# Moving VectorE's maxima ahead of its transposes, and with them the order of a transfer queue, in a two-layer cross-attention kernel

## The chip, the cores and the metric

The kernel runs on one core of a Trainium2 chip. The metric is the device time of one launch in microseconds (us). Engines go by the names of the profile: PE is the matrix engine TensorE (PEld its weight loads), DVE is VectorE, ACT is ScalarE, POOL is GpSimd, and SP is SyncE, which here issues nearly all DMA transfers. Each engine works through its own instructions in order, and waits on semaphores for the others.

## What is computed

The reference, cut to its parts (16 batches, 256 rows of width 256, all float32):

```
x = x + L0_xattn(ctx, LN(x))   # 8 heads of 128; queries from LN(LN(x)); keys and values
                               # over the 512 rows LN(ctx) and LN(LN(x))
x = x + L0_ffn(LN(x))          # 256 -> 1024 -> 256, GELU; both weights get an update
                               # per batch, products of tokens 1..16 of the batch
x = x + L1_xattn(LN(x), ctx)   # one head of 256, keys and values from ctx
x = x + L1_moe(LN(x))          # 8 experts (gate, up, down, width 256); weights by a
                               # sigmoid zone, with a fallback to the top two
```

## The kernel before, in words

**Two kinds of work.** The first attention is laid out head by head: 16 batches of 8 heads give 128 heads, and the loop at L1239 to L1279 runs a step n for each (and two more). Everything else of a batch is its *tail*: the FFN, the second attention and the routing (`chain`, L332, and `route`, L584). The experts (`experts`, L1174) begin to run near the end of the loop. Tails are generators: each `yield` ends a unit, and says how many microseconds of PE time should pass before the next one. The step calls `gap()` (L114), which runs units of tails that are due by a clock (`Clock.pe`) that sums the modelled time of matmuls. So the order on every engine is fixed when the program is built; at run time the engines only wait for each other. The chain of batch b-1 joins in at head 2 of batch b.

**A head.** Its steps are spread over several steps of the loop, so that PE always has another head's work:

- `s0q(n+1)` (L801) and `s0k(n+1)` (L814): query and key projections `pq`, `pk`; their results `qT`, `kT` are evicted by ACT (`evict`, L774), or by DVE while the clock says that ACT is taken.
- `s1(n)` (L832): for both halves of the queries the scores `sc`, on DVE the maxima `nm` (L841), on ACT the exp into `pr` (L847).
- `s1_scale(n)`: reciprocals on DVE (L854), scaling of `pr` on POOL (L855).
- `s2(n)` (L857): DVE transposes `pr` in blocks of 32 into `tb` (L863, a single buffer), and SP writes `tb` to DRAM: `hop`, 512 KB (L867).
- `s2_fetch(n)` (L870): SP reads it back in another order, four transfers of 128 KB, into `pT` (L876, two buffers).
- `s3(n)` (L879): PE multiplies `pT` with the values into `po`, and DVE evicts it as `outT` (L893).

Step n of the loop calls, in this order: `s1(n)`, a gap, `s1_scale(n)`, `s2_fetch(n-1)`, `s0q(n+1)`, a gap, `s0k(n+1)`, gaps with `bulk` between them, `s3(n-2)`, a gap, `s2(n)`. `bulk` (L1010) advances the values' projection `pv` and `inputs(b+1)` (L714): the statistics, normalized rows (`cn`, `xn`) and, by DVE transposes and trips through DRAM (`hop_cin`, `hop_cn`, `hop_xn`, fetched into `raw`), the transposed inputs `kvT` of the next batch. It advances the inputs at heads 0 to 4.

**A tail, as far as the change touches it.** The output projection `px` (L351) is added to x (L354); statistics follow, and the reciprocal deviation `rs_b` on POOL (L262). DVE normalizes to `yb` (L267) and copies a few rows to `yp` (L373). SP writes 8 rows to DRAM (`ev_d`, two transfers of 4 KB, L375 and L376) and reads them back to all partitions, `ev`, 1 MB (L380): these are the weight rows from which the FFN's updated weights are made. Then `to_blocks` (L285 to L296) transposes `yb` on DVE and writes it to DRAM, `hop_yb` (256 KB), fetched by `from_blocks` (L299) in four transfers. After the FFN comes the second attention in the same manner: `yc` and its `hop_yc`, the queries' constants `rc` (two reductions on DVE, L488), the values `pv1` (L500), the queries `q1T` from the fetched `ycT` (L508), scores and exp, `pr1` through DRAM (`hop_pr`, `pr1T`), its copy `pT1` (L537), the product `po1`, statistics and `rs_d`. Last comes `row` (L557), which needs `rs_d`, and its own trip, for the routing and the experts.

Since SP has one queue for all of this, a fetch stands behind every transfer issued before it.

Of the kernel before, what the change touches and what calls it, by code (L numbers as in the profile page):

```python
# [16 lines left out]
ALU = mybir.AluOpType  # L17
# [12 lines left out]
def xattn_ffn_kernel(  # L30
# [10 lines left out]
    nc = tc.nc  # L41
    B, S, D = x.shape
# [7 lines left out]
    TC = S // P  # L50
# [13 lines left out]
    wk = ctx.enter_context(tc.tile_pool(name="work_c", bufs=1))  # L64
# [49 lines left out]
    def gap(least=0.8, stand=0.0):  # L114


        t = Clock.pe
        while Clock.pe - t < least:
            line[:] = [j for j in line if not j.done]
            if not line:  # L120
                return
            job = next((j for j in line if j.ready <= Clock.pe), None)
            if job is None:
                soon = min(j.ready for j in line)
                if soon > Clock.pe + stand:
                    return
                Clock.pe = soon
                continue
            job.unit()
        line[:] = [j for j in line if not j.done]  # L130
# [15 lines left out]
        out=before, in_=before, compare_op=ALU.is_gt, fill=0.0,  # L146
# [9 lines left out]
        out=below, in_=below, compare_op=ALU.is_gt, fill=0.0,  # L156
# [77 lines left out]
    g1 = keep.tile([P, D], F32, name="g1")  # L234
    g0 = keep.tile([P, 1], F32, name="g0")
# [49 lines left out]
    def to_blocks(pool, src, C, tag, bufs, name, most=None):  # L285
        tb = pool.tile(
            [P, C * D], F32, tag=tag, bufs=bufs, name=name, padded_shape=[P, most or C * D]
        )
        tb = tb.rearrange("p (m d c s) -> p m d c s", m=QP, d=DC, c=C)
        for c in range(C):  # L290
            nc.vector.transpose(  # L291
                tb.rearrange("p m d c s -> p d m c s")[:, :, :, c, :],
                src[:, c, 0:D].rearrange("p (d m r) -> p d m r", d=DC, m=QP),
            )
        hop = dram.tile([P, QP, DC * C * QB], F32, tag=f"{tag}{C}", name=f"hop_{name}")
        nc.sync.dma_start(hop, tb.rearrange("p m d c s -> p m (d c s)"))  # L296
        return hop
# [11 lines left out]
    SENT, LANDED = 6.5, 7.5  # L309
# [22 lines left out]
    def chain(b, A, behind):  # L332
# [37 lines left out]
        y = wk.tile([P, TC, D], F32, tag="y", name=f"yb_{b}")  # L370
        ln_apply(y, x_b, mv, rs)
        yp = wk.tile([32, NI, NA], F32, tag="yp", name=f"yp_{b}")
        nc.vector.tensor_copy(yp, y[0:32, 0, :].rearrange("p (a c) -> p c a", c=NI))  # L373
        ev_d = dram.tile([2 * NI, D], F32, tag="ev_d", name=f"ev_d_{b}")
        nc.sync.dma_start(ev_d[0:NI, :], y[1 : 2 * NI : 2, 0, :])  # L375
        nc.sync.dma_start(  # L376
# [6 lines left out]
        )  # L383
        landed = Clock.pe + 15.0
        plus_row(x_b, lasting["b2"])
        hop = to_blocks(wk, y, TC, "tbc", 1, f"yb_{b}_b")
        yield SENT
        yTb = raw_tile("yT", f"ybT_{b}")
        from_blocks(yTb, hop)
# [94 lines left out]
        hop = to_blocks(wk, y, TC, "tbc", 1, f"yc_{b}_b")  # L484
        pr = wk.tile([P, TC, S], F32, tag="pr1", name=f"pr1_{b}")
        rc = small.tile([P, TC], F32, tag="rc", bufs=2, name=f"rc_{b}")
        for c in range(TC):
            nc.vector.tensor_tensor_reduce(  # L488
                out=pr[:, c, :], in0=y[:, c, :], in1=g1, op0=ALU.mult, op1=ALU.add,
                scale=1.0, scalar=g0, accum_out=rc[:, c : c + 1],  # L490
            )
        yield SENT
        yTc = raw_tile("raw_c", f"ycT_{b}")
        from_blocks(yTc, hop)
        landed = Clock.pe + LANDED


        v1 = wk.tile([P, TC, D], F32, tag="v1", name=f"v1_{b}")
        for m in range(TC):
            pv = mm_tile(D, f"pv1_{b}_{m}")  # L500
            for d in range(DC):
                mm(pv, cT[:, d, ts(m, P)], WvT[:, d, :], start=(d == 0), stop=(d == DC - 1))
            evict(v1[:, m, :], pv, None, None)
            yield
        yield landed - Clock.pe
        q1T = wk.tile([P, DC, S], F32, tag="q1T", name=f"q1T_{b}")
        for m in range(DC):
# [27 lines left out]
        pT = wk.tile([P, TC, S], F32, tag="pT1", bufs=1, name=f"pT1_{b}")  # L535
        for m in range(TC):
            evict(pT[:, m, :], in_order(raw)[:, m], None, None)  # L537
        yield 2.5
        mv = mv_tile("d")
        for c in range(TC):  # L540
            ri = small.tile([P, 1], F32, tag="ri1", name=f"ri1_{b}_{c}")
# [9 lines left out]

        rs = ln_rstd(mv, "d")
        nc.sync.dma_start(out[b].rearrange("(c p) d -> p c d", p=P), x_b)
        yield 2.8
        while b >= 2 and not A.tails[b - 2].done:
            yield 0.4
        row = A.row[b] = wk.tile([P, TC, ROW], F32, tag="row", bufs=2, name=f"row_{b}")  # L557
# [136 lines left out]
    with ExitStack() as sh, ExitStack() as sa, ExitStack() as sf:  # L694
# [137 lines left out]
        def s1(n):  # L832

            b, h = divmod(n, H)
            qT, kT = heads[n]
            rows_ = []
            for c in range(TC):
                sc = psum.tile([P, J], F32, tag="sc", name=f"sc_{b}_{h}_{c}")
                mm(sc, qT[:, ts(c, P)], kT, start=True, stop=True)
                nm = small.tile([P, 1], F32, tag="nm", name=f"nm_{b}_{h}_{c}")  # L840
                nc.vector.tensor_reduce(nm, sc, AX.X, ALU.max, negate=True)  # L841
                rows_.append((sc, nm))
            heads[n] = []
            for c, (sc, nm) in enumerate(rows_):
                pr = wh.tile([P, J], F32, tag="pr", bufs=4, name=f"pr_{b}_{h}_{c}")
                sm = small.tile([P, 1], F32, tag="sm", name=f"sm_{b}_{h}_{c}")
                nc.scalar.activation(pr, sc, AF.Exp, bias=nm, accum_out=sm)  # L847
                heads[n].append((pr, sm))
# [21 lines left out]
        def s2_fetch(n):  # L870

            b, h = divmod(n, H)
            pT = wh.tile([P, QP, TC, P], F32, tag="pT", name=f"pT_{b}_{h}")
            from_ = heads[n].rearrange("(a r) m f -> m r a f", r=QB)
            for m in range(QP):
                nc.sync.dma_start(pT[ts(m, QB)].rearrange("r a c f -> r a (c f)"), from_[m])  # L876
            heads[n] = pT

        def s3(n):  # L879

            b, h = divmod(n, H)
            pT, v = heads.pop(n), A.v[b, h // HG]
            o = wh.tile([P, S], F32, tag="outT", bufs=H + H // 2, name=f"outT_{b}_{h}")
            A.outT.setdefault(b, []).append(o)
            po = mm_tile(S, f"po_{b}_{h}")
            for j in range(JC):
                mm(
                    po, v[:, j, ts(h % HG, DH)],
                    pT.rearrange("p a c f -> p c a f")[:, :, :, ts(j, QB)],
                    start=(j == 0), stop=(j == JC - 1),  # L890
                )

            nc.vector.tensor_scalar(o, po, col("bv", h), None, ALU.add)  # L893
# [116 lines left out]
        def bulk(b, h):  # L1010
            if h == 0:
                if b == 0:
                    filling["turns"] = all_turns()
                filling["in"] = inputs(b + 1) if b + 1 < B else None
            if h == 2:
                filling["v1"] = values(b, 1)
            if h == 6:
                filling["v0"] = values(b + 1, 0) if b + 1 < B else None
            if b == 0:
                load_late(h)  # L1020
                for _ in range(2):
                    advance(filling["turns"])
            if 2 <= h <= 5:
                advance(filling["v1"])
            if h <= 4:
                advance(filling["in"])
            if h == 7 and b + 2 < B:
                load_in(b + 2)
            if h >= 6:
                advance(filling["v0"])  # L1030
                yield
                advance(filling["v0"])
            yield
# [205 lines left out]
        for n in range(NS + 2):  # L1239
            b, h = divmod(n, H)  # L1240
            if h == 2 and b > 0:
                last = add_chain(b - 1, last)
            more = bulk(b, h) if n < NS else None
            if n < NS:
                s1(n)
            if n == NS - 4:
                sf.close()
                open_front()
                rest = Job(experts(
                    lists,  # L1250
                    lambda g: g.part == 0 or B - 1 in A.tails and A.tails[B - 1].done,
                ))
                line.append(rest)
            if n == NS - 1:
                sa.close()
                open_last_layer()
            while behind_exp:
                behind_exp.pop()()
            stand = 2.0 if n >= NS - 1 else 0.0
            gap(stand=stand)  # L1260
            if n < NS:
                s1_scale(n)
            if 1 <= n <= NS:
                s2_fetch(n - 1)
            if n + 1 < NS:
                s0q(n + 1)
            gap(stand=stand)
            if n + 1 < NS:
                s0k(n + 1)
            gap(stand=stand)  # L1270
            advance(more)
            gap(stand=stand)
            advance(more)
            gap(stand=stand)
            if n >= 2:
                s3(n - 2)
            gap(stand=stand)
            if n < NS:
                s2(n)  # L1279
        line.remove(rest)  # L1280
        last = add_chain(B - 1, last)
        line.append(rest)
# [56 lines left out]
```

## Time and profile before

| | |
|---|---|
| median of 3 runs | 1907.38 us (1905.83 to 1913.34) |
| the profiled execution: its time, its span | 1906.59 us, 1904.8 us |
| mean granted clock of PE | 0.989 |
| PE busy | 1824.0 us, 96% of the span |
| PE weight loads, DVE | 1228.8 us (65%), 1226.8 us (64%) |
| ACT, POOL | 593.1 us (31%), 871.1 us (46%) |
| DMA | 336.92 MB, mean 177 GB/s; SP's queue took 47.1% of the 16 DMA engines' span |
| largest single transfers | `ev` 1024 KB (16 times), `hop` 512 KB (128 times), `pT` 128 KB (512 times) |

A row of groups names the source line, the engine, the operation with output and inputs, the tile shapes and the count; behind the first bar are busy time and mean nanoseconds of one, and behind the second the idle time of the engine just before such instructions, with what ended most of it. In a timeline the columns are start and duration in us, engine, line, operation, count (x2 is two run together), and in brackets a wait before it and its releaser. Engine SPq is the issue of a transfer by SP, not the transfer itself. All matmuls carry line L80, that of the helper that issues them, so they are told apart by their tiles.

### The profile page before, as it was taken

The page shows a single profiled execution, that of the slowest core. Times are in us where ns is not written, and L with a number is a line of the kernel's source. Part 1 is how long each engine was busy: PE and PEld are TensorE (multiplying, and loading weights), DVE is VectorE, ACT ScalarE, POOL GpSimd, SP SyncE. Part 2 cuts the span into 40 slices and gives each one's busy share as a digit, 9 for nine tenths or more (in the row PEclk, how much of TensorE's full clock was granted, in tenths as well). Part 3 has the DMA queues.
Part 4 walks back from the last instruction along what each step waited for, and adds up shares of the span by engine and source line. Part 5 has one row for each costly group of instructions (what it writes and reads, how often), then busy time and mean ns, then how long its engine had stood idle before and what let it go on. Part 6 is the DMA issues. An engine that isn't in the chain of part 4 may idle for free. (4 is left out here: it accounts for less than half of the span.)

```text
span 1904.8 us, 22785 instructions
## 1 busy us (share of the span) xinstructions
PE 1824.0 (96%) x6568; PEld 1228.8 (65%) x6568; DVE 1226.8 (64%) x3324; ACT 593.1 (31%) x1323; POOL 871.1 (46%) x996
## 2 busy tenths in 40 slices
PE   8999999999999999999999999999999999899996
PEld 4666666666666666666666666666666767566665
DVE  4466586757575757585857575858574767565654
ACT  3433334333333333333333333333333212111110
POOL 2132226343535353535353535353534275767666
PEclk9999999999999999999999999999999999999999
DMA  6553536464636463636363636363636587999996
GB/s 214 177 188 122 167 133 216 140 200 136 200 131 204 133 213 130 199 126 212 128 216 128 212 127 203 126 214 126 219 118 202 157 224 194 232 246 234 216 206 109
DMA packets 274638, 336.92 MB, mean 177 GB/s; under 512 B 31772, under 2 KB 227272, under 8 KB 272456
## 3 DMA queue, kind: packets, MB, share of 16 engines
q1 hardware_dynamic: 243736, 283.82, 47.1%
q0 software_dynamic: 30720, 51.54, 11.4%
q8 instruction: 55, 0.90, 0.2%
q14 instruction: 79, 0.65, 0.1%
q10 hardware_dynamic: 48, 0.01, 0.0%
HBM read 167.87 MB, written 167.38 MB: 176 GB/s over the span
## 5 line engine op out<-in xcount | busy, mean ns | idle before, releaser
L855 POOL TENSOR_SCALAR pr<-pr,ri 128x512 f32<-128x512 f32 x256 | 182.5, 725 | 664.0 <-DVE ri L854 662.0
L847 ACT ACTIVATE pr<-sc,nm 128x512 f32<-128x512 f32 x256 | 173.5, 682 | 578.1 <-DVE nm L841 575.4
L674 POOL DMA_INDIRECT slots_d<-row,at_slot x256 | 255.6, 998 | 68.2 <-issue 68.2
L80 PE MATMUL sc<-kT,qT 128*128 128x512 f32 x512 | 253.1, 618 | 33.2 <-ACT kT L780 33.2
L80 PE MATMUL po<-pT,v 128*128 128x256 f32 x1024 | 243.3, 380 | 4.0 <-DMA pT<-hop 3.6
L1165 POOL DMA_INDIRECT out_dram<-o,at x128 | 200.0, 1563 | 99.2 <-DVE o L1164 27.1
L80 PE MATMUL pk<-kvT,Wk_sb 128*128 128x512 f32 x512 | 240.6, 592 | 0.0
L80 PE MATMUL pv<-Wv_sb,kvT 128*128 128x512 f32 x512 | 239.1, 596 | 0.1
L80 PEld LDWEIGHTS po<-pT,v 128*128 128x128 f32 x1024 | 194.4, 190 | 67.0 <-issue 37.7
L863 DVE STREAM_TRANSPOSE tb<-pr 128x512 f32<-128x512 f32 x256 | 165.6, 684 | 34.9 <-DMA hop<-tb 34.9
L80 PEld LDWEIGHTS sc<-kT,qT 128*128 128x128 f32 x512 | 98.0, 197 | 108.7 <-issue 64.8
L841 DVE TENSOR_REDUCE nm<-sc 128x1 f32<-128x512 f32 x256 | 160.3, 662 | 4.8 <-PE sc L80 3.8
L893 DVE TENSOR_SCALAR outT<-po,cvec 128x256 f32<-128x256 f32 x128 | 60.0, 469 | 157.8 <-PE po L80 137.6
L80 PEld LDWEIGHTS pv<-Wv_sb,kvT 128*128 128x128 f32 x512 | 95.6, 190 | 98.4 <-issue 89.0
L80 PEld LDWEIGHTS pk<-kvT,Wk_sb 128*128 128x128 f32 x512 | 97.3, 190 | 67.8 <-issue 61.2
L80 PE MATMUL pd<-wx,hTd 128*128 128x256 f32 x512 | 125.8, 383 | 9.9 <-DVE hTd L1151 7.9
L80 PE MATMUL pq<-kvT,Wq_sb 128*128 128x256 f32 x512 | 131.9, 380 | 0.0
L1140 ACT ACTIVATE sg<-pg 128x384 f32<-128x384 f32 (+3 forms) x82 | 41.2, 503 | 290.6 <-PE pg L80 242.8
L80 PE MATMUL pg<-yTd,wx 128*128 128x384 f32 (+3 forms) x328 | 125.1, 504 | 3.6 <-issue 3.0
L80 PEld LDWEIGHTS pq<-kvT,Wq_sb 128*128 128x128 f32 x512 | 97.5, 191 | 42.9 <-issue 31.3
L80 PEld LDWEIGHTS pd<-wx,hTd 128*128 128x128 f32 x512 | 97.4, 192 | 41.8 <-DVE hTd L1151 8.7
L80 PE MATMUL pu<-yTd,wx 128*128 128x384 f32 (+3 forms) x328 | 124.4, 502 | 0.0
(191 smaller groups left out, 2703.2 us busy)
## 6 DMA issues: line engine op xcount, KB each, us to landing
hop<-tb SPq DMA_DIRECT2D x128, 512.0 KB
pT<-hop SPq DMA_DIRECT2D x512, 128.0 KB
ev<-ev_d SPq DMA_DIRECT2D x16, 1024.0 KB
rows<-slots_d SPq DMA_DIRECT2D x31, 397.5 KB
hop_rows_b<-rows_b SPq DMA_DIRECT2D x30, 384.0 KB
yTd<-hop_rows_b SPq DMA_DIRECT2D x120, 96.0 KB
rows<-slots_d SPq DMA_DIRECT2D x8, 530.0 KB
cin<-in_ctx_dram SPq DMA_DIRECT2D x16, 256.0 KB
```

Source lines behind the costliest of these rows:

```text
L80: nc.tensor.matmul(out, lhsT, rhs, **kw)
L674: ins = nc.gpsimd.indirect_dma_start(out=slots_d[part], out_offset=bass.IndirectOffsetOnAxis(ap=at_slot[:, c, e : e + 1], axis=0), in_=row ...
L841: nc.vector.tensor_reduce(nm, sc, AX.X, ALU.max, negate=True)
L847: nc.scalar.activation(pr, sc, AF.Exp, bias=nm, accum_out=sm)
L855: nc.gpsimd.tensor_scalar(pr, pr, ri, 1.0, ALU.mult, ALU.mult)
L863: nc.vector.transpose(tb[:, :, c, :], heads[n][c][0].rearrange("p (m f) -> p m f", m=QP))
L893: nc.vector.tensor_scalar(o, po, col("bv", h), None, ALU.add)
L1140: nc.scalar.activation(self.sg, self.pg, AF.Tanh, scale=0.5)
L1165: ins = nc.gpsimd.indirect_dma_start(out=out_rows[0 : sum(NTOKS[: self.part + 1]), :], out_offset=bass.IndirectOffsetOnAxis(ap=self.at[:, ...
```

## The change

Seven edits; the number of instructions of each kind stays what it was.

1. `s2(n-1)` is called in step n right after `s1(n)`, where before `s2(n)` ended step n. The maxima of head n so come ahead of the transposes of head n-1.
2. `s2_fetch(n-1)` moves from after `s1_scale(n)` to after `s3(n-2)`, near the end of the step.
3. `inputs` is advanced at heads 1 to 5 instead of 0 to 4.
4. The queries' constants `rc` are computed after the values `v1` (two units later), and the queries' `landed` time is set 1.5 later.
5. The product `po1` is due 4.0 instead of 2.5 after `pT1`.
6. The tail's `hop_yb` (transposes and write) comes ahead of `ev_d` and `ev` on DVE and SP.
7. In the last batch `row` is due 10.0 instead of 2.8 after `rs_d`.

In the built program one more thing follows from the clock: in twelve batches the two copies into `ydT` are DVE's instead of ACT's.

```diff
         nc.vector.tensor_copy(yp, y[0:32, 0, :].rearrange("p (a c) -> p c a", c=NI))
+        hop = to_blocks(wk, y, TC, "tbc", 1, f"yb_{b}_b")
         ev_d = dram.tile([2 * NI, D], F32, tag="ev_d", name=f"ev_d_{b}")
...
         landed = Clock.pe + 15.0
         plus_row(x_b, lasting["b2"])
-        hop = to_blocks(wk, y, TC, "tbc", 1, f"yb_{b}_b")
         yield SENT
...
         rc = small.tile([P, TC], F32, tag="rc", bufs=2, name=f"rc_{b}")
-        for c in range(TC):
-            nc.vector.tensor_tensor_reduce(
-                out=pr[:, c, :], in0=y[:, c, :], in1=g1, op0=ALU.mult, op1=ALU.add,
-                scale=1.0, scalar=g0, accum_out=rc[:, c : c + 1],
-            )
         yield SENT
         yTc = raw_tile("raw_c", f"ycT_{b}")
         from_blocks(yTc, hop)
-        landed = Clock.pe + LANDED
+        landed = Clock.pe + LANDED + 1.5
...
             evict(v1[:, m, :], pv, None, None)
             yield
+        for c in range(TC):
+            nc.vector.tensor_tensor_reduce(
...
         yield landed - Clock.pe
...
             evict(pT[:, m, :], in_order(raw)[:, m], None, None)
-        yield 2.5
+        yield 4.0
...
         nc.sync.dma_start(out[b].rearrange("(c p) d -> p c d", p=P), x_b)
-        yield 2.8
+
+        yield 2.8 if b < B - 1 else 10.0
...
-            if h <= 4:
+            if 1 <= h <= 5:
                 advance(filling["in"])
...
             if n < NS:
                 s1(n)
+            if 1 <= n <= NS:
+                s2(n - 1)
...
             if n < NS:
                 s1_scale(n)
-            if 1 <= n <= NS:
-                s2_fetch(n - 1)
...
             if n >= 2:
                 s3(n - 2)
+            if 1 <= n <= NS:
+                s2_fetch(n - 1)
             gap(stand=stand)
-            if n < NS:
-                s2(n)
```

More of the change, by code (lines that the diff above doesn't have):

```diff
@@ L504, in chain @@
             yield
+        for c in range(TC):
+            nc.vector.tensor_tensor_reduce(
+                out=pr[:, c, :], in0=y[:, c, :], in1=g1, op0=ALU.mult, op1=ALU.add,
+                scale=1.0, scalar=g0, accum_out=rc[:, c : c + 1],
+            )
         yield landed - Clock.pe
```

## The prediction, made before the changed kernel ran

> **What bounds the kernel now.** I read four views in this order: busy shares and groups, the waits of TensorE (PE), the timeline of one batch, and the window table where PE had waited. PE is busy 1824.0 of 1904.8 us, so only what makes PE wait, or slows its clock, moves the time. Its groups:
>
> ```profile
> L80 PE MATMUL sc<-kT,qT 128*128 128x512 f32 x512 | 253.1, 618 | 33.2 <-ACT kT L780 33.2
> L80 PE MATMUL po<-pT,v 128*128 128x256 f32 x1024 | 243.3, 380 | 4.0 <-DMA pT<-hop 3.6
> ```
>
> The last columns are the idle time before the group and what ended it. Scores wait 33.2 us for keys evicted by ScalarE; the weighted values wait 4.0 us although every head's `pT` goes out to DRAM and back. The waits, as sum, count, longest:
>
> ```profile
> PE sc L80 <- ACT kT L780: 33.2, 13, 2.8
> PE pd L80 <- DVE hTd L1151: 7.9, 2, 7.7
> PE po L80 <- DMA pT<-hop: 3.6, 4, 2.5
> PE po L80 <- ACT pT L778: 3.1, 4, 1.2
> ```
>
> The 13 waits are twelve of 2.2 to 2.8 us, one a batch from batch 4 on, always ahead of head 2's scores, and one of 1.5. In batch 9:
>
> ```profile
> 843.30 1.96 PE L80 MATMUL sc<-kT,qT 128*128 128x512 f32 x4
> ...
> 846.55 1.02 DVE L488 CUSTOM_DVE_ANT_0 pr<-yc,g,g 128x256 f32<-128x256 f32 x1
> 847.91 1.29 DVE L863 STREAM_TRANSPOSE tb<-pr 128x512 f32<-128x512 f32 x2
> 849.13 1.25 DVE L841 TENSOR_REDUCE nm<-sc 128x1 f32<-128x512 f32 x2
> 849.88 0.69 ACT L847 ACTIVATE pr<-sc,nm 128x512 f32<-128x512 f32 x1 [7.77 <-DVE nm L841]
> 851.57 0.69 ACT L780 ACTIVATE kT<-pk,cvec 128x512 f32<-128x512 f32 x1
> 852.32 1.98 PE L80 MATMUL sc<-kT,qT 128*128 128x512 f32 x4 [2.74 <-ACT kT L780]
> ```
>
> Head 1's scores are done by 845.3, but VectorE (DVE) first works off inputs, the constants (L488) and the transposes of head 0, and takes the maxima at 849.13. ScalarE stands in order behind its exp, so head 2's keys come 3.2 us after that and PE 2.74 us late. The releaser ACT is innocent; DVE's order is the cause.
>
> **The change, part by part.**
>
> *Maxima first, constants and inputs later: gain.* Built, the maxima of head n stand ahead of head n-1's transposes. In the odd batches what remains ahead of head 1's maxima is nine routing rows (2.27 us in batch 9), in the even ones less. The maxima then start about 2.9 us after the scores instead of 849.13-843.30 = 5.83; keys follow 3.19 us later (852.32-849.13), at 6.1; PE has work until 849.58, 6.3 after them. The wait goes, by 0.2 us in odd batches, amply in even ones: -33.2. What was ahead is late next: the transposes of head 0 (1.29) only have to be in DRAM a head (12 us) later, the constants (two units later, 1.36) before the last cross-attention's maxima, the inputs a head later but a batch ahead of use. DVE is 64% busy; priced 0 (exposed, +1.3 us a batch, 20). Transposes wait 34.9 us in all for their single buffer's hop; that now falls behind the maxima, so it stops nobody.
>
> *The clock after those waits.* One of them:
>
> ```profile
> 755.00:756.00 1.00, 0.34 (x1) 0.35 (x2) 0.93 (x5) 0.60 (x2) 0.83 (x2) 0.63 0.00 0
> 756.00:757.00 1.00, 1.00 (x2) 0.48 (x2) 1.00 (x4) 0.00 (x0) 0.93 (x1) 0.50 0.45 153
> ```
>
> Columns: length, PE, its weight loads, DVE, ACT, POOL, clock, DMA, GB/s. After six of the twelve waits the clock is 0.50 for some 3.4 us, so 1.65 us are lost; after the other six nothing. "TensorE: Matmul & The Clock Gate" in the Trainium skill ("Why this matters for your kernels") asks only that PE never idles over about 3 us; by that rule 2.2 to 2.8 us cost no clock and the gain is 33. By the row it is 33.2 + 6 x 1.65 = 43. I take the row: -9.9.
>
> *`s2_fetch` to the end of the step: the cost.* The four `pT` transfers of head n-1 (512 KB) now go to SP's queue behind all that tail jobs and inputs issue in that step. At most heads little is there. But at head 2 the FFN tail's `ev` broadcast (1 MB) lies in this very step, with `hop_yb` (256 KB) now ahead of it. In the built order `ev` precedes head 2's `pT` in every batch; before, from batch 2 on, `pT` preceded it. Batch 1 of before shows that order:
>
> ```profile
> 121.95 0.33 SPq L380 DMA_DIRECT2D ev<-ev_d  x1
> 122.38 0.38 SPq L296 DMA_DIRECT2D hop_yb_b<-yb_b  x1
> 122.86 2.14 SPq L876 DMA_DIRECT2D pT<-hop  x4
> ...
> 130.31 0.89 PE L80 MATMUL po<-pT,v 128*128 128x256 f32 x3 [0.33 <-DMA pT<-hop]
> ```
>
> 1.75 MB were in 8.36 us after `ev` was issued, and PE already waited 0.33 for them. Batch 9 shows a follower's price too: `pr1T`, issued behind `ev`, held ACT 2.36 us:
>
> ```profile
> 877.90 0.73 DVE L267 TENSOR_SCALAR yb<-x,mv_b,rs_b 128x256 f32<-128x256 f32 x2 [1.15 <-POOL rs_b L262]
> 881.40 0.35 SPq L380 DMA_DIRECT2D ev<-ev_d  x1
> 891.35 0.71 ACT L778 COPY pT<-pr1T 128x256 f32<-128x256 f32 x2 [2.36 <-DMA pr1T<-hop_pr_b]
> ```
>
> The time left, counted from the end of `px` (875.44 in batch 9). There are two patterns. In eight batches (2, 3 and the odd ones) inputs' `xn` and its transposes (1.11 + 0.77) come between the statistics and `yb`, partly in the 1.15 us wait for `rs_b`: +0.7. Then `yp` 0.37, the transposes 0.75 and the hop's issue 0.38 stand before `ev_d`: +1.5. `ev`, at 5.96 before, goes out at 8.2. Behind it are 1 MB and 0.5 MB of `pT`: scaled from 8.36, 7.2 us; with all of `hop_yb` still ahead, 8.4 (1.75 MB as in the row). Landing at 15.4 to 16.6; PE needs `pT` at 11.2 (pk, pv, po of head 1, sc, pq, pk, pv, at their rows' durations). Wait 4.2 to 5.4; I take 4.6, as part of `hop_yb` has drained in the 2.2 us that `ev_d` takes. In six batches (4, 6 .. 14) `ev` goes out at 7.9 and another 0.5 MB (`raw`, `hop_xn`) stand between: 9.6 to 10.7, landing 17.5 to 18.6, needed at 12.0 (one projection more): 5.4 to 6.6; I take 5.6. Lower bound: at the 279 GB/s that the window from 123 to 124 us shows under `ev` (DMA share 1.03), plus about 1 us at the end, 3.4 and 4.1, so 52. Sum 8 x 4.6 + 6 x 5.6 = 70. PE has nothing else in its order; the maxima, the exp and the next heads queue behind. The three other waits of this trace above 2.4 us (2.45 at 1468, 2.96 at 1540, 7.72 at 1652) are all followed by a clock of 0.50, so I add 14 x 1.5 = 21. Together +91; bounds 52 + 10 = 62 and 8 x 5.4 + 6 x 6.6 + 24 = 107.
>
> Here a rule and the row differ. "DMA: Bandwidth & Descriptors" in the Trainium skill ("Where 436 GB/s comes from") gives a ceiling of 435 GB/s for a core's 16 engines. By it 1.5 and 2.0 MB take 3.4 and 4.6 us, landing with 1 us at the end at 12.6 and 13.5: waits of 1.4 and 1.5, 20 in all and no clock lost, so an estimate of -35 for the whole change. By the row it is 1.75 MB in 8.36, half that rate, and +91 for this part. The row has the very transfers in the very order; I take it.
>
> *Queries later.* `q1T` waits for `ycT` 4.4 us in all (the same view) and `landed` is 1.5 us later, but `ycT` is fetched behind one more hop: 0, bounds -4 and +4. `pT1` units of 4.0 instead of 2.5: its waits for ACT (3.1) go, as 1.5 us is above the longest, 1.2: -3.1. The copies of `ydT` of twelve batches move from ACT to DVE by the clock of the planner, 0.8 us each batch under 10 us of PE work: 0.
>
> *Last batch.* The row's wait before the end:
>
> ```profile
> 1657.46 0.74 DVE L267 TENSOR_SCALAR row<-x,mv_d,rs_d 128x256 f32<-128x256 f32 x2 [11.86 <-POOL rs_d L262]
> 1660.10 2.93 PE L80 MATMUL pd<-wx,hTd 128*128 128x256 f32 x6 [7.72 <-DVE hTd L1151]
> ```
>
> DVE stands before `rs_d`, which queues on POOL behind scatters; the experts' products behind it on DVE leave PE idle 7.72 us. Putting the row 7.2 us of PE work later leaves about 4.6 of DVE's wait and 0.5 of PE's: -8.5 with some of the dip; bounds 0 and -9.5 (a dip more). Batch 0 gets its `pT` behind Wo's 1 MB: +2.
>
> Sum: 91 - 33.2 - 9.9 - 3.1 - 8.5 + 2 = +38; less 2 for the earlier waits for `pT` that these take over: +36. On the profiled execution's 1906.6 us this is 1943; the median is 0.8 above it, inside its scatter.
>
> **Rivals.**
> *The fetch lands in time* (not slower). If `ev` reaches the queue sooner, or `pT`'s share of the engines isn't behind all of it, no wait arises: -33.2 - 9.9 - 3.1 - 8.5 = -55, 1852. Point of decision: landing 11.2 (12.0) us after `px`, that is, 3 to 4 us after `ev`'s issue; batch 1's 8.36 speaks against it. For it: only four waits for `pT` in 128 heads so far, and 400 GB/s in some windows. With waits of up to 2.4 us, and so up to 34, this is still faster: 1852 to 1897. Chance 0.2.
> *Waits that cancel the gain.* 3.2 us each with half the dips: 14 x 3.2 + 10 = 55, about 1907. Chance 0.12.
> *Every head late.* Some `pT` waits are 0.3 to 0.45 us now; if each of 128 heads gets 0.45 more on top of +36, +58: 2000. In the trace hops land several us ahead at most heads. Chance 0.05.
> *The change doesn't do what it says*: the wait before head 2 stays at odd batches, where the margin is 0.2 us. Six waits of about 1 us: +6, inside the main case.
>
> **Numbers.** Main case 0.63: 1943; its range 62 - 45 = +17 to 107 - 40 = +67, so 1924 to 1974 (45 and 40 are the reliefs with the queries' bounds). A measurement of this kernel tells 0.5% (9.5 us) from no change. The range wanted reaches into the rivals: from 1880, where about 0.12 lies below, to 1974, 0.06 above. Faster 0.21, same 0.11, slower 0.68.
>
> **What would show it.** Right: the scores' wait for ACT `kT` falls from 33.2 below 3; PE's waits for DMA `pT<-hop` rise from 3.6 to some 70, one a batch, at head 2, each followed by clock 0.50; `ev` before `pT` on SP's queue; the row's wait falls from 11.9 to about 5. Wrong: waits for `pT` staying below 20, or DMA hops landing within 4 us of `ev`; or the wait for `kT` merely moving to another head.

## The result, and the profile after

The changed kernel took 1959.23 us (median of 4 runs, 1956.96 to 1965.75) against 1910.36 us for the kernel before on the same chip: a ratio of 1.0262, 95% interval 1.0224 to 1.0299, so some 50 us slower. The profiled execution has a span of 1957.9 us, 53.1 more than before. PE's busy time rose by 22.8 us (1824.0 to 1846.8) and its idle time by 30.3; the mean clock fell from 0.989 to 0.970.

The two groups of the page shown in the prediction, after:

```profile
L80 PE MATMUL po<-pT,v 128*128 128x256 f32 x1024 | 270.2, 411 | 78.8 <-DMA pT<-hop 78.8
...
L80 PE MATMUL sc<-kT,qT 128*128 128x512 f32 x512 | 254.3, 621 | 0.0
```

The scores' 33.2 us are gone to the last tenth, and the weighted values wait 78.8 instead of 4.0. They also got slower: 411 ns each instead of 380, because what follows such a wait runs at half clock. PE's waits (sum, count, longest):

```profile
PE po L80 <- DMA pT<-hop: 78.8, 18, 6.4
PE pg L80 <- DMA yTd<-hop_rows_b: 7.9, 1, 7.9
...
PE pg L80 <- DVE o L1165: 3.3, 2, 2.7
...
PE pq L80 <- DMA ycT<-hop_yc_b: 0.4, 1, 0.4
```

Of the 18 waits for `pT`, 14 are 4.2 to 6.4 us, one in each of batches 2 to 15, ahead of head 2's product. Batch 9 in the timeline:

```profile
903.79 0.42 DVE L354 TENSOR_TENSOR x<-px,x 128x256 f32<-128x256 f32 x1 [1.64 <-PE px L80]
904.81 0.70 DVE L267 TENSOR_SCALAR xn<-x,mv_x,v 128x256 f32<-128x256 f32 x2
907.08 0.75 DVE L291 STREAM_TRANSPOSE yb_b<-yb 128x256 f32<-128x256 f32 x2
907.86 0.34 SPq L296 DMA_DIRECT2D hop_yb_b<-yb_b  x1
911.06 0.33 SPq L381 DMA_DIRECT2D ev<-ev_d  x1
911.49 1.80 SPq L877 DMA_DIRECT2D pT<-hop  x4
919.13 3.75 PE L80 MATMUL po<-pT,v 128*128 128x256 f32 x8 [4.20 <-DMA pT<-hop]
```

Read it downwards: `xn` and two sets of transposes stand between the statistics and `ev`; `pT` is issued 0.4 us behind `ev`; PE had finished at 914.93 and starts at 919.13, 8.07 us after `ev`'s issue. The product then takes 3.75 us instead of the 1.9 of a product at full clock. The clock by windows (sixth value behind the length; in brackets the counts):

```profile
918.00:919.00 1.00, 0.00 (x0) 0.00 (x0) 0.00 (x0) 0.00 (x0) 0.00 (x0) 0.75 1.05 319
...
921.00:922.00 1.00, 1.00 (x4) 0.82 (x3) 0.00 (x0) 0.14 (x1) 0.00 (x0) 0.50 1.15 291
...
924.00:925.00 1.00, 1.00 (x2) 0.34 (x1) 0.37 (x1) 0.00 (x0) 0.00 (x0) 0.50 0.66 206
925.00:926.00 1.00, 1.00 (x4) 0.49 (x3) 0.40 (x2) 0.58 (x1) 0.00 (x0) 0.83 0.76 253
```

Half clock lasts from about 918.5 to 925.3, 6.8 us, twice the 3.4 of the stretches behind the scores' waits before. Half clock followed each of the 14 waits for 6.8 us.

The end of the last batch:

```profile
1709.69 0.74 DVE L267 TENSOR_SCALAR row<-x,mv_d,rs_d 128x256 f32<-128x256 f32 x2 [2.59 <-POOL rs_d L262]
...
1794.00 0.37 SPq L1083 DMA_DIRECT2D rows<-slots_d  x1
...
1799.71 2.90 PE L80 MATMUL pg<-yTd,wx 128*128 128x384 f32 x4 [7.85 <-DMA yTd<-hop_rows_b]
```

The row waits 2.59 instead of 11.86 us, and the 7.72 us at `pd` are gone; but 90 us later PE waits 7.85 us at `pg`. Ahead of that SP stood from 1778.3 to 1794.00, 15.2 us of it for the last batch's scatters to land (the last of them ran on POOL until 1792.15), with the fetches for the experts behind it.

### The profile page after: what moved, and what is told of

Its sections match the earlier page's. It is cut to its first block, busy times and chain, and to the rows that moved or that the text cites. A ratio compares the mean times of both kernels' runs of the same rounds, so it can differ in the third digit from the quotient of the medians.

```text
span 1957.9 us, 22743 instructions
## 1 busy us (share of the span) xinstructions
PE 1846.8 (94%) x6568; PEld 1248.3 (64%) x6568; DVE 1225.6 (63%) x3348; ACT 602.0 (31%) x1299; POOL 878.5 (45%) x996
## 4 chain that ended last, share of the span: by engine, by line
PE 82%; DMA 8%; DVE 4%; POOL 2%; issue 2%; SPq 1%; ACT 0%; ACTq 0%; POOLq 0%; DVEq 0%
PE po L80 13%; PE sc L80 11%; PE pv L80 10%; PE pk L80 9%; PE pq L80 6%; PE ph L80 6%; PE pf L80 6%; PE pg L80 5%; PE pu L80 5%; PE px L80 5%; PE pd L80 5%; DMA pT<-hop 4%; DMA raw<-hop_cn 1%; DMA ev<-ev_d 1%; SPq L877 1%
## 5 line engine op out<-in xcount | busy, mean ns | idle before, releaser
L856 POOL TENSOR_SCALAR pr<-pr,ri 128x512 f32<-128x512 f32 x256 | 189.3, 750 | 651.7 <-DVE ri L855 647.9
L80 PE MATMUL po<-pT,v 128*128 128x256 f32 x1024 | 270.2, 411 | 78.8 <-DMA pT<-hop 78.8
L80 PEld LDWEIGHTS po<-pT,v 128*128 128x128 f32 x1024 | 207.5, 206 | 145.7 <-issue 107.0
L842 DVE TENSOR_REDUCE nm<-sc 128x1 f32<-128x512 f32 x256 | 172.5, 684 | 63.7 <-PE sc L80 59.2
L80 PEld LDWEIGHTS sc<-kT,qT 128*128 128x128 f32 x512 | 104.3, 204 | 77.1 <-issue 68.4
L779 ACT COPY v<-pv 128x512 f32<-128x512 f32 (+1 forms) x132 | 70.5, 534 | 205.5 <-PE pv L80 180.8
```

The lines of the kernel that those rows point to most:

```text
L80: nc.tensor.matmul(out, lhsT, rhs, **kw)
L779: nc.scalar.copy(out, src)
L856: nc.gpsimd.tensor_scalar(pr, pr, ri, 1.0, ALU.mult, ALU.mult)
```

## Experiments

**Theory**: head 2's `pT` comes late since its fetch moved behind the tail's 1 MB `ev` on SP's queue; waits and half clock together are the loss. **Rivals**: the transposes, put behind the maxima, send the hop too late; the end of a step is too late by itself; and, for the gains, a wait that goes comes back elsewhere. Every time is a median of 4 or more runs; ratios are to the kernel before on the same chip, in brackets the 95% interval.

**fetch_early**: the changed kernel with the fetch at its old place.

```diff
                 s1_scale(n)
+            if 1 <= n <= NS:
+                s2_fetch(n - 1)
...
                 s3(n - 2)
-            if 1 <= n <= NS:
-                s2_fetch(n - 1)
```

> The changed kernel with the one edit of the fetch undone: the fetch of a head's pT stands again right after the scaling, ahead of the tail's ev. Theory (ev ahead of head 2's pT on SP's queue is the whole loss): PE's waits for DMA pT fall from 78.8 to under 8, the fifteen stretches at half clock that follow them go, and the time is 1959 - 73 - 27 = about 1860. Rival (the transposes, now behind the maxima, send the hop off too late, whatever the queue): waits for pT of 2 us or more stay at many heads, time above 1920.

Measured 1910.18 us, ratio 0.9999 (0.9985 to 1.0013). Undoing that one edit takes off 49 us: waits for `pT` fell to 25.1, and half clock became rarer than before. But nothing is left of the 55 us that the prediction gives the other edits:

```profile
PE po L80 <- DMA pT<-hop: 25.1, 14, 5.4
PE po L80 <- ACT pT L779: 14.2, 7, 2.3
PE pg L80 <- DVE o L1165: 9.4, 1, 9.4
...
PE ph L80 <- ACT v L779: 4.2, 6, 0.7
```

The first line is now head 3, not head 2. In batch 9:

```profile
884.31 0.33 SPq L381 DMA_DIRECT2D ev<-ev_d  x1
...
887.03 0.37 SPq L868 DMA_DIRECT2D hop<-tb  x1
893.39 1.73 SPq L877 DMA_DIRECT2D pT<-hop  x4
...
897.71 1.97 PE L80 MATMUL po<-pT,v 128*128 128x256 f32 x8 [1.75 <-DMA pT<-hop]
```

Head 3's *write* is behind `ev` now. Its fetch, which has to wait until it has landed, is issued 6.4 us after it, where 2.7 is the median over the heads of the kernel before. So `ev` delays this follower as it delayed the other.

**no_ev**: the changed kernel, but the broadcast is sent in batch 0 only.

```diff
-        ev = wk.tile([P, 2 * NI, D], F32, tag="ev", name=f"ev_{b}")
+        ev = A.ev if b > 0 else wk.tile([P, 2 * NI, D], F32, tag="ev", name=f"ev_{b}")
+        A.ev = ev
...
+        if b == 0:
             nc.sync.dma_start(
                 ev.rearrange("p n d -> p (n d)"),
```

> The changed kernel without the 1 MB broadcast from batch 1 on (the weight rows of batch 0 are used again, so the first FFN's update is that of another batch; all instructions on the compute engines stay). Theory (the bytes of ev and SP's stand before it are what head 2's pT waits for): waits for pT fall from 78.8 to under 12 and the half-clock stretches with them: 1959 - 68 - 25 = about 1866. Rival (the fetch at the step's end is too late by itself): at least 2 us a batch stay, 1920 or more.

Measured 1873.13 us, ratio 0.983 (0.9799 to 0.986). With the fetch at the step's end, 83 (by the ratios) to 86 us (by the times) of the changed kernel's time hang on `ev`. The waits for `pT` fell, though not below the 12 expected:

```profile
PE po L80 <- DMA pT<-hop: 18.5, 11, 3.5
```

Without `ev` the late fetch still costs 1.6 to 2.4 us in every second batch, where `raw` and `hop_xn` lie between `ev_d` and it, so the rival "too late by itself" holds a small part.

**ev_behind**: the changed kernel, `ev` issued right after the step's fetch.

```diff
+        def send_rows():
             nc.sync.dma_start(
                 ev.rearrange("p n d -> p (n d)"),
...
+        if b < B - 1:
+            rows_due.append(send_rows)
+        else:
+            send_rows()
...
                 s2_fetch(n - 1)
+            while rows_due:
+                rows_due.pop()()
```

> The changed kernel with all its edits, but the 1 MB ev broadcast is issued right after the fetch of that step instead of ahead of it. Theory: head 2's pT no longer has 1 MB ahead of it, its landing comes 4 to 5 us earlier, waits for pT fall from 78.8 to under 15, time 1860 to 1875. Rival (the end of a step is too late for a fetch, with ev or without): waits of 2 us or more remain at head 2 of most batches, time above 1920.

Measured 1936.91 us, ratio 1.0118 (1.0079 to 1.0158). The time is the rival's, but at head 2 neither expectation holds: waits of 2 us or more remain there, but in four batches only. Two of the lines say where the time went:

```profile
PE po L80 <- DMA pT<-hop: 50.7, 22, 7.2
PE po L80 <- DVE W1e L411: 10.6, 3, 6.1
```

Head 2 waits 1.6 to 4.3 us in the even batches from 4 on and at most 0.5 in the others, instead of 4.2 to 6.4, but `pT` of head 3, with its hop, is now the one behind `ev`, 1.9 to 7.2 us late, and the weight rows themselves come late for `W1e`. "`ev` ahead of `pT`" was too narrow: in batch 9 of the changed kernel SP issues 3.25 MB in 12 us (901.41 to 913.34, from `hop` to `pr1T`), which at the 0.3 MB/us of its windows takes 11. A fetch that has only 3.4 us until it is needed (911.49 to 914.93) finds no good place in that; before, it was issued some 9 us earlier.

**fetch_late_only**: the kernel before with the fetch's move alone.

> The kernel before with the fetch's move alone. Theory: ev (issued 6.0 us after px), hop_yb, then pT, as in batch 1: landing 14.3 after px, needed at 11.2 to 12.0: waits for pT of 2.5 to 3 us, 14 times, 38 in all, and some 14 half-clock stretches of 1.5 to 2.5; the scores' waits of 33 stay: 1910 + 38 + 28 = about 1976, at least above 1940. Rival (the fetch's place costs nothing unless DVE's order changes too): 1910.

Measured 1992.78 us, ratio 1.0426 (1.0403 to 1.045), slower than the whole change:

```profile
PE po L80 <- DMA pT<-hop: 72.3, 30, 4.2
PE sc L80 <- ACT kT L780: 20.6, 13, 2.2
PE pq L80 <- DMA ycT<-hop_yc_b: 10.9, 10, 2.0
```

Head 2 waits 3.7 to 4.2 us from batch 2 on, more than the 2.5 to 3 expected (I had not counted what `hop_pr` and `raw` leave in the queue ahead of `ev`; how much of the 1 us that is was not taken apart). A second wait, of 0.6 to 1.8 us, is at head 0, and `ycT`, fetched later, adds 6.5. Alone the edit costs 82 us, more than the 49 that the whole change loses.

**maxima_first_only**: the kernel before with the move of `s2` alone.

> The kernel before with the move of the transposes behind the next head's maxima alone (inputs, constants, fetch, hop_yb as before). Theory: the transposes of head 0 (1.29 us) no longer stand ahead of head 1's maxima, but inputs and constants still do: the score's waits of 2.2 to 2.8 us shrink by 1.3 to some 1.4, so 17 to 20 of the 33 go, and the half-clock stretches after them: 1910 - 17 - 10 = about 1883. Rival (the transposes are the whole of it): waits near 0 and 1867.

Measured 1949.06 us, ratio 1.0197 (1.0173 to 1.022). The scores' waits shrank as expected (33.2 to 19.1, twelve of them 1.0 to 1.7), yet it is 38 us slower:

```profile
PE pq L80 <- DMA ycT<-hop_yc_b: 36.8, 13, 4.1
PE sc L80 <- ACT kT L780: 19.1, 13, 1.7
PE po L80 <- ACT pT L778: 13.0, 12, 2.2
```

SP works in order, and a hop's issue waits for its transposes. In batch 9:

```profile
882.79 0.38 SPq L867 DMA_DIRECT2D hop<-tb  x1
883.26 3.20 SPq L302 DMA_DIRECT2D ycT<-hop_yc_b  x4
...
889.94 3.43 PE L80 MATMUL pq<-ycT,M 128*128 128x256 f32 x8 [4.14 <-DMA ycT<-hop_yc_b]
```

`ycT` is queued behind head 1's hop. Since that hop's transposes now follow the next head's maxima, `ycT` goes out later too, and lands 2.4 to 4.1 us too late in twelve batches. The change shows only 0.4 us here. Its later `landed` is the likely reason, but no run takes that out alone.

**inputs_constants_later**: the kernel before with edits 3 and 4 alone, without the 1.5 in `landed`.

> The kernel before with inputs a head later and the queries' constants two units later alone; transposes, fetch, hop_yb and due times as before. Theory (DVE's queue ahead of head 1's maxima sets the 33 us): 1.8 + 1.36 = 3.2 us leave that queue, more than the 2.2 to 2.8 of the wait, so it goes, with its half-clock stretches: 1910 - 33 - 10 = about 1867. Rival (what leaves the scores comes back as another wait, as with the fetch put early): 1895 to 1910.

Measured 1885.9 us, ratio 0.989 (0.9863 to 0.9918), between the two expectations: the scores' wait fell to 10.1, 0.8 each, and no half clock followed any of them. But 6.6 us of new waits for `hT` stand at `pv`, and the waits of `po1` for ACT rose from 3.1 to 6.9.

**fetch_mid**: the changed kernel, `s2_fetch(n-1)` right after `s0k(n+1)`.

> The changed kernel with the fetch between its two places: after the key projection, so ahead of yb and ev, but some 4 us behind its own hop's issue, which SP then need not stand for. Theory: waits for pT under 12, and fewer of the new waits for pT1 than with the fetch put early: 1860 to 1885. Rival (the gain is spent elsewhere whatever the place): 1900 to 1910.

Measured 1884.41 us, ratio 0.9881 (0.9853 to 0.9908). The time is in the range expected. Waits for `pT` are 15.4 instead of under 12, and those of `po1` for ACT 3.1 where fetch_early has 14.2. `pT` is ahead of `ev`. SP still stands 278 us in all for hops before their fetches (295 with the fetch early), so what makes this place the better one was not taken apart.

**hop_behind_ev**: the changed kernel without edit 6.

> The changed kernel with hop_yb behind ev again. Theory: ev is issued 1.1 to 1.5 us earlier (transposes 0.75, issue 0.38) but hop_yb's 256 KB now lie between ev and pT, about 0.8 us at the rate seen: a wait 0.3 to 0.7 us shorter in 14 batches, 1950 to 1958. Rival (hop_yb's place is a main part of the loss): below 1940.

Measured 1939.23 us, ratio 1.0171 (1.0139 to 1.0203): 17 (by the ratios) to 20 us (by the times) better than the change, so the rival is nearer. Its waits are 62.7 us in all: in the odd batches from 3 on they became 3.2 to 3.9 from 4.2 to 4.8, in the even ones from 4 on 4.5 to 4.9 from 5.5 to 6.4. Part of the gain is the clock. In batch 9 (a wait of 3.35, from 900.52 to 903.87), in windows cut where the clock changes (their grid is explained below):

```profile
900.50:903.92 3.42, 0.07 (x2) 0.08 (x1) 0.00 (x0) 1.57 (x3) 2.28 (x3) 1.00 1.09 341
903.92:907.33 3.41, 3.41 (x8) 2.71 (x9) 0.00 (x0) 0.71 (x2) 0.00 (x0) 0.50 1.02 343
907.33:910.75 3.42, 3.42 (x11) 1.90 (x10) 2.65 (x5) 1.47 (x5) 0.00 (x0) 1.00 0.56 172
```

Half clock lasts 3.4 us where the change has 6.8.

**last_row_early** (the change without edit 7), **mid_and_row_early** (fetch_mid without it), **mid_row_early_hop_behind** (fetch_mid without it and edit 6), **later_and_po1** (inputs_constants_later and edit 5):

> The changed kernel with the last batch's row due 2.8 after rs_d, as before. The prediction's step (the later row saves 8.5 us): 1959 + 8 = 1967. Rival (the later row only moves the stall: the last batch's scatters end later on POOL, and the rows that SP reads from them hold the last experts, 7.85 us at pg): the wait for pd of some 7 comes back, the wait at pg goes, 1957 to 1961.

> The kernel with the fetch after the key projection (all other edits of the change), and the last row due 2.8. If the later row saves 8.5 us: 1884 + 8 = 1892. If it only moves the stall, which measured 9.7 us at pg there against 6.5 to 7.7 at pd: 1881 to 1884.

> The same with hop_yb behind ev as well. With pT ahead of ev in the queue hop_yb's place should no longer matter to pT: theory 1880 to 1885, within 3 us of the kernel before it in this list. Rival (hop_yb ahead of ev costs by itself): 10 us or more faster.

> The kernel before with inputs a head later, constants two units later, and po1 due 4.0 after pT1. The pT1 waits for ACT (6.9 us, 9 times) go: 1886 - 7 = 1879. Rival (each wait that goes comes back in another place): 1884 to 1888.

| kernel | us | ratio (95%) |
|---|---|---|
| last_row_early | 1959.49 | 1.0258 (1.023 to 1.0286) |
| mid_and_row_early | 1882.46 | 0.9851 (0.9823 to 0.9878) |
| mid_row_early_hop_behind | 1886.76 | 0.9879 (0.9848 to 0.991) |
| later_and_po1 | 1876.49 | 0.9817 (0.9789 to 0.9846) |

Edit 7 saves nothing: in last_row_early the wait at `pd` is back and the one at `pg` gone.

```profile
PE pd L80 <- DVE hTd L1152: 7.2, 2, 7.0
```

With `pT` ahead of `ev`, `hop_yb`'s place shows no difference clear of the noise (1882 and 1887, intervals overlapping). later_and_po1 beats both kernels; transposes and fetch stay where they were. Its lines:

```profile
PE pv L80 <- ACT qT L780: 8.7, 6, 1.6
...
PE po L80 <- DMA pT<-hop: 7.4, 9, 2.6
...
PE sc L80 <- ACT kT L780: 4.9, 6, 0.8
```

The waits of `po1` for ACT are gone (6.9 to 0.2), and the scores' halved; at `pv` 8.7 for `qT` came in the place of the 6.6 for `hT`.

## Why the prediction was right, point by point

The direction and the cause were right; the loss was put at 36 us and measured at some 50, and most of the difference is in one term.

- **Waits for `pT`.** Predicted 4.6 in eight batches and 5.6 in six, 70 in all. Measured over the same batches 4.7 and 5.7, 71.9. Single steps were off and cancelled: `ev` went out 7.5 us after `px`, not 8.2 (DVE filled the wait for `rs_b` better), `pT` landed 8.1 us after it where 7.2 to 8.4 was reckoned. The estimate from a ceiling of 435 GB/s ("DMA: Bandwidth & Descriptors" in the Trainium skill, "Where 436 GB/s comes from"), -35 us for the change, was far off: 1.5 MB took 8.07 us, and the windows from 912 to 919 us show 303 to 346 GB/s, one of them 136. fetch_early and no_ev show the cause. ev_behind corrects its wording: it is the load of the queue in that stretch, with fetches issued late, and not one transfer ahead of another.
- **The clock: the term that was mis-sized.** I put each wait at one stretch, 1.5 us, 14 x 1.5 = 21, net +11. Weighing each 1 us window's missing clock with PE's busy share gives 14.3 us lost before and 41.7 after: +27, of which 22.8 show as busy time. Each of the 14 waits was followed by 6.8 us of half clock, twice as long (2.3 to 3.1 us lost). The trace before held one wait as long, 7.72 us, and its windows showed half clock from 1656 to 1663; I counted it as one stretch of 3.4 us, though it was as long as two. (A wait of 7.45 us at the very start, with no half clock behind it, I passed over.) What decides between one stretch and two is told below the list.
- **The scores' waits.** -33.2 as predicted, also in the odd batches, where the margin was put at 0.2 us, and with them went the six half-clock stretches.
- **"It stops nobody": transposes behind the maxima at 0.** Right for the changed kernel and wrong as a step. maxima_first_only shows 32 us more of waits at `ycT` (4.4 to 36.8): I had followed the transposes on DVE, but not the hop that they hold on SP nor the fetches queued behind it. What paid for it in the change is likely the queries' later due time, which I priced at 0; no run isolates that.
- **`po1`.** -3.1 as predicted. **`q1T`**: -4.0, at the edge of its bounds.
- **Last batch: -8.5 was wrong.** The row did get early (11.86 to 2.59, I said 4.6) and `pd`'s wait went, but the stall moved to `pg`; the tail's waits went from 13.4 to 12.5. I asked what would follow the row on DVE and not what its scatters would hold on POOL and SP.
- **Sum.** Waits: +25 predicted, +30 measured. Clock: +11 and +23. The main case's range was worked wrongly: the reliefs listed come to 55, and with the bounds of the queries and of the row to 42 to 60, not to 40 and 45, which puts its ends at 1909 and 1972 instead of 1924 and 1974. The measured time lies in both.
- **The rival "lands in time"**, 1852, could not have come true by the fetch alone. With the fetch early the other edits bring nothing, with it in the middle 23 to 28 us. So their 55 us were not free to take: much of what PE no longer waits for at one place it waits for at the next.

**One stretch of half clock or two.** The length of a wait does not decide this alone. In each of the 14 traces all half-clock stretches begin on one grid: they lie whole multiples of 3.413 us apart, to within 0.002 us, and all but the last, which runs to the end, take one, two or three slots of that length. Two waits of fetch_late_only, in windows cut at the slots, first 4.13 us (223.07 to 227.21), then 3.83 us (934.26 to 938.08):

```profile
223.84:227.25 3.41, 0.04 (x1) 0.07 (x1) 0.00 (x0) 1.44 (x4) 0.00 (x0) 1.00 1.02 326
227.25:230.66 3.41, 3.41 (x8) 2.74 (x9) 0.00 (x0) 0.00 (x0) 0.00 (x0) 0.50 0.79 227
230.66:234.08 3.42, 3.42 (x11) 1.90 (x10) 2.88 (x6) 0.82 (x3) 0.00 (x0) 1.00 0.45 162
...
933.81:937.22 3.41, 0.45 (x2) 0.00 (x0) 0.00 (x0) 2.17 (x5) 0.00 (x0) 1.00 1.05 348
937.22:940.63 3.41, 2.55 (x6) 2.13 (x7) 0.00 (x0) 0.71 (x2) 0.00 (x0) 0.50 0.89 278
940.63:944.05 3.42, 3.42 (x6) 1.74 (x6) 2.16 (x4) 0.00 (x0) 0.00 (x0) 0.50 0.48 156
```

The longer wait ends just before a new slot, PE works through all of that slot, and half clock lasts one slot. The shorter ends 0.86 us into a slot, and half clock lasts two. Counted over all 14 traces (from 8 us on, without the stretch at the end): a slot at full clock in which PE idled 2.0 us or more was followed by half clock in all 126 cases, one with 1.92 us or less in none. A slot at half clock with 0.63 us or more idle was followed by another in all 78 cases, one with 0.62 us or less by full clock in all 133.

So waits of one length can cost differently. In the kernel before, six of the twelve waits of 2.2 to 2.8 us put 2.0 us or more into one slot, and these six had the stretch behind them. Of the fourteen waits of 3.7 to 4.2 us in fetch_late_only nine cost two slots and five one. In the change a batch takes 29 slots (its stretches come 98.99 us apart), so its waits fell on the grid much alike, with 0.63 us or more of each in the first slot at half clock. That all fourteen cost two is in part where they fell, and that the prediction could not know: the grid lies differently against the start of each trace, by up to 2.8 us.

What stays open: how much of the change's small wait for `ycT` is owed to the later due time, why the fetch in the middle is 26 us better than early, and why leaving out edit 6 shortened the waits by 0.9 to 1.5 us where 0.3 to 0.7 was expected.

## What to carry to other kernels

A queue that issues in order makes every move of a transfer, or of what a transfer waits for, a move of all that is queued behind it: price a moved step by walking each queue that it feeds, and note for the followers when they are needed. A wait costs more than its length where the clock reacts: find the grid of its stretches in the trace, cut the waits at its slots, and, as a new kernel's waits may fall elsewhere on it, price both one slot and two. And a wait at the end of a chain of equals is worth removing only if the next one in line has slack; here delaying two unneeded pieces of DVE work gave 1.1%, with one later due time 1.8%, while reordering the engine and the queue cost 2.6%.

## What the runs showed of the hardware

Half clock came in slots of 3.413 us, on a grid fixed within a trace: it always began after a slot with 2.0 us or more of PE idle, never after one with 1.92 or less, and ended after the first slot with at most 0.62 us idle. A fetch that follows its own write at once on SP is issued 2.7 us after the write's issue (median over the heads before) and, behind the 1 MB broadcast in fetch_early, 6.4. The small trip through DRAM ahead of `ev` (two transfers of 4 KB) holds SP 2.2 us (908.90 to 911.06) before the broadcast can be issued.
